# Two graph layers on 128 small graphs: attention weights of the end groups normalised by two engines, one add for two token halves, and new tables for the order of the engines

## The chip, the core and the metric

The kernel runs on one core of a Trainium2 chip. A core has a matrix engine (TensorE, PE in the profile, with its weight loads as PEld), VectorE (DVE), ScalarE (ACT), GpSimd (POOL), and SyncE (SP), whose queue issues the DMAs here. TensorE writes to PSUM[...]. The metric is the device time of one execution in microseconds (us); lower is better.

## The reference, cut to what matters

128 graphs of 128 nodes with 256 features, all fp32, go through two layers. The first has two graph attentions, a layer norm, a feed-forward network and another layer norm; the second has eight-head attention masked by relation, a projection, a layer norm, a feed-forward network and a layer norm.

```python
# layer 0: twice _gat, then layer norm, feed-forward, layer norm
Wh = jnp.matmul(h, W)
e = jax.nn.leaky_relu(Wh @ a1 + swap(Wh @ a2))
att = softmax(where(adj > 0, e, -9e15), axis=1)
h = jnp.matmul(att, Wh)
ff = relu(h @ w_ff1 + b_ff1) @ w_ff2 + b_ff2
# layer 1
attn = softmax(q @ k.T / sqrt(32), axis=-1)
out = sum over r of (attn * (adj == r)) @ v_r
x = _ln(src + out @ Wo + bo)
ff = gelu(x @ W1 + b1) @ W2 + b2
return _ln(x + ff)
```

`adj` holds only 0 and 1. The kernel counts that on the chip and takes a branch for it: two relations instead of four.

## The kernel before, in words

**Tiling.** The 128 graphs make 32 groups of four. In each group one graph's 128 nodes lie on the 128 partitions; `y` is a tile of 128 x 4 x 256. A token of the code below (index `b` or `j`) is one of the four graphs of a group. A group passes five stages: `load` (DMAs of the transposed input `xt` and the mask `at`), `gat` (two graph attentions and a normalisation), `ff0`, `att` (eight heads, two graphs at a time) and `ff1` with the store. Affine parts of the layer norms are applied on GpSimd (L591).

**Feed-forward.** Both products are done as seven block products (the Strassen-Winograd scheme), each part with sums made by VectorE and GpSimd. The first product (L658) runs in two units of four visits each: u0a, u0b, u1a, u0c and so on. A visit ends with an add on VectorE (L665, L674, L675) and a copy on ScalarE (L664, L669, L670) of the same PSUM bank, which a later visit writes again. The second product (L714) adds its results to `y` through `add` (L719) in seven steps; the last is added to both halves of the output columns of tokens 2 and 3. Then `normalised` follows: bn_stats (L577), bn_aggr (L578), an epsilon add (L580), a power on GpSimd (L582), the negative mean (nmr, L583), and four scaled copies on ScalarE (L585).

**Attention weights.** For two graphs at a time the scores (L849) go to PSUM, VectorE takes the row maxima (L853), ScalarE the exponentials with their sums (L862), VectorE the reciprocals (L864), and GpSimd multiplies the 128 x 1024 tile `e` by them (L865). Then `e` is transposed: in the middle groups through VectorE's 32 x 32 transpose (L608) and DRAM, by four stores (L611) and one load (L617) on SyncE's queue; in groups 0 and 31 (`direct`) on TensorE (L602), with copies out of PSUM by ScalarE (L606) and VectorE (L604). The feature tiles `T` are turned in the same two ways. The mask multiply (L884) follows on VectorE, the weighted sums (L913) and the output product (L940) on TensorE.

**Graph attention.** `gat_weighting` needs one column of `wh` as a row on every partition: VectorE transposes it (`zs`, L761), SyncE stores it (`zsd`, L763) and loads it back on all partitions (L766). ScalarE adds the column (L769), VectorE does the leaky step (L776), the mask (L777) and the maximum (L778), ScalarE the exponentials (L781), VectorE the reciprocal (L782), GpSimd the multiply (L783). `cap` (L789) is the compare of the mask.

**What sets the order.** Each stage is a generator that yields between steps. `run` takes the steps of all groups from a heap by their times: a period of 100 per group, a `begin` for each stage, and a list of waits (`steps`). Instructions on TensorE and SyncE keep the order of their steps. Each instruction on VectorE (V), ScalarE (S) and GpSimd (G) has a lag of its own in a table; sorting by step time plus lag gives the order in which its engine gets it, and this order is fixed by dependencies. The numbers are only for sorting: they are not device time. Groups 0 and 31 have tables of their own. A first part, with its own table (`PREFIX`), does the graph attention of groups 0 to 2 and the first feed-forward of group 0, prepares weights, and scans the adjacency (L1113 on ScalarE, L1116 on VectorE); at its end a flag is read and the branch is taken, near 95 us of the profile.

Of the kernel before, what the change touches and what calls it, by code (L numbers as in the profile page):

```python
# [25 lines left out]
G = 4  # L26
# [25 lines left out]
    begin=dict(load=-119.75, gat=-11.95, ff0=94.95, att=174.9, ff1=347.7),  # L52
    steps=dict(
        load=(
            84.25,
        ),
        gat=(
            3.6, 5.8, 1.7, 17.4, 23.25, 4.55, 12.25, 11.5, 16.85,
        ),
        ff0=(  # L60
            1.45, 19.1, 6.85, 4.85, 5.95, 3.1, 5.95, 0.1, 0.3, 0.5, 0.6, 0.4, 0.3, 0.25, 17.5, 0.2,
            0.3,
        ),
        att=(
            2.8, 17.5, 4.45, 19.45, 0.15, 0.55, 0.35, 31.6, 22.6, 0.3, 0.45, 2.45, 5.7, 22.3, 14.15,
# [3 lines left out]
            19.2, 2.9, 3.6, 3.85, 8.5, 0.35, 2.45, 2.05, 0.25, 2.8, 0.15, 1.7, 0.35, 17.9, 4.1, 1.65,  # L69
            37.65, 48, 8, 5.75,  # L70
# [3 lines left out]
        (-2, "ff1"): -2, (-1, "load"): -2, (-1, "ff1"): -5, (3, "load"): 24, (-4, "load"): -10,  # L74
        (4, "load"): -7, (5, "load"): -1, (-5, "load"): -6,
# [3 lines left out]
V 15.2 | S 104.7 95  # L79
S 102.8 104.1  # L80
V 99.9
|
V 102.7 104.7 105.4 117.1 | S 110.4 110.8 110.6 106 112.8 113.3 111.3 112.7 | G 113.4
S 97.7 98.3 99.6 100.4
V 96.7
|
V 84.8 85.6 88.4 99.3 | S 84.3 87.2 88.1 86.4 96.8 90.8 90.2 98.2 | G 102.7
V 91.7 93 92.1 92.3 93.3 95.1 96.7 97.9 98 98.2 98.4 98.6 | S 102.1 99.8 99.4 97 | G 100.7
""",
        "ff0": """  # L90
V 95.8
|
G 92.7 103.2 97.6 110.4
V 107.9 | S 107.3
S 104.3 104.8
V 102.9 | S 103.6 | G 54.9 67.7
V 103.6 104.5
S 98.8 100.9 | G 48.3 50.9
S 103.9 99.6 100.9 105 102.3 98.5
V 101.1 103.3  # L100
S 104.4 106.1 105.3 105.9 106.7 104.2
|
V 101.6 104.3 | G 106.4 100.5
V 105.4 107 | G 110.3
V 105.3 108.1 108.5 | G 104.5
V 96.3 97.5
V 100.9
V 104.4 105.5 100.6 101.4 101.5 106 106.2 107 106.6 107.1 107.3 108.7 | S 111.8 112.5 114.6 110.7 | G 107.2
# [4 lines left out]
V 106.7 105 | S 102.9 114  # L113
V 103.9 106.2 107.4 108.2 110.6 117.5 | S 110.9 112.3 112.9 114.7 113.6 116 115.6 116.9 116.9 121.2 117.3 119.6 120.1 120.9 119.5 120.3 | G 110.5 119.3
V 96.6 103
|
V 110.5 112 | G 55.4 67
V 122.1 129.6
V 105.4 105.6 107.4 107.6 111.5 115.5 | S 104.5 107 108.4 107.3 108.7 108.8 109.6 109 109.9 110.5 114.3 113.2 113.6 110.2 112 113.5 115.4 | G 111.2 116.4
V 97  # L120
V 92.1 95.8
|
V 96.8 98.8 | G 9 14.1
V 106.8 108.6
S 119.4
V 105.5
V 45.9 54.2 50.8 59.3 99.3 99.9 99.7 100 100.5 102.8 | S 103.8 104 105.6 104.7 | G 97.4
""",
        "ff1": """
V 87.7  # L130
|
G 96.4 96.4 111.7 103.9
V 94.9 | S 93.9
S 100.6 92.2
V 92.8 | S 93.3 | G 48.2 62.3
V 96.3 103
S 93.3 93.9 | G 43.6 51.8
S 101.5 102.2 96.5 102.9 90.8 104.9
V 98.6 101.8
S 102.4 102.7 102 102.9 99.4 101.4  # L140
|
V 100 107 | G 92.1 106.8
V 99.7 111.4 | G 101
V 94.7 96 99.5 | G 92.2
V 97.3 100.3
V 101.3
V 65.3 67.6 64.2 64.3 66.8 68.5 70.1 72.5 70.2 72.4 74.1 75.6 | S 77.5 80.2 78.3 76.4 | G 70.5
G 34.5 80.5
G 45.7 46.4
""",  # L150
        "ff0 -1": """
V 100.1 | S 97.2
|
G 71.5 75.6 91.9 103.7
V 109.3 | S 106.9
S 104.2 106.8
V 102.4 | S 101.1 | G 68 76.2
V 105.3 101.8
S 95.4 97.11 | G 59 72.5
S 96.8 99 101.8 104.5 101.3 96  # L160
V 100.8 102.3
S 107.5 110.3 110 110.3 104.5 105.8
|
V 99.5 101.1 | G 102 107.7
V 104.2 109.7 | G 112.9
V 109.6 110.6 113.1 | G 107
V 100.1 101.3
V 101.17
V 103.9 105.7 100.99 102.2 102.1 102.6 105.9 107.2 106.1 106.48 107.8 111 | S 105.12 106.3 106.55 106.8 | G 111
""",  # L170
        "att 0": """
V 119.5 111.85 113.2 113.3 114.4 120.5 116.2 114.8 103.4 109.5 120.6 128.2 107.7 119 112.8 | S 142.2
|
V 105.3 103.7 | S 125.3 129.53
V 105.7 111.1 113 113.3 116.2 119.6 | S 125.46 125.69 125.91 126.9 126.6 126.6 126.82 127.28 127.05 129 127.2 128.2 127.5 128.9 128.64 128.87 | G 109.3 111.2
V 102.2 109.9 | S 110.35 118.1
|
V 103 112.3 | G 66.7 80.2
V 101.7 115
V 102.6 105.9 106.2 107.57 109.2 120.2 | S 98.4 101.2 103 100.3 100.9 102.6 106.3 104.6 111.7 104.4 107 113.3 114 107.7 114.3 115.1 116.9 | G 105.5 121.2  # L180
V 95.8
V 97.05 108.1 | S 102.7 120.3
|
V 104.6 115 | G 12.3 13.3
V 99.4 100
S 112
V 101.3
V 43.7 48 44.1 52.4 95.45 96.2 95.8 97.5 98.61 104.5 | S 105 109.5 109.2 108.7 | G 97
""",
        "att -1": """  # L190
V 101.6 | S 108.7
|
V 106.8 95.7 | S 101.3 101.8
V 103.2 105.6 106 106.5 112 115.8 | S 98.6 102.7 101.6 103.7 104.7 107.8 105.8 110.9 107.4 111 111.5 120 113.1 116.2 112.1 113.7 | G 111 115.6
V 99.3 101.74 | S 102.6 106.2
|
V 108.3 110.8 | G 60.1 61.3
V 99.2 102.1
V 90.2 93.7 96.7 103.7 104.7 107.2 | S 84.3 90.9 95.5 90.7 93.8 102.6 104.2 94.9 98.5 104.3 107.4 97.6 105.2 104.5 110.1 106.8 111.4 | G 90.7 96.2
V 85.8  # L200
V 98 89.3 | S 90.1 93
|
V 95.3 110.7 | G 2 6.7
V 89.8 103.6
S 93.9
V 101.8
V 43.19 53 43.6 45.4 97.3 101.93 101.85 102 102.5 103.1 | S 84.8 87.7 94 104.3 | G 92.5
""",
        "ff1 0": """
V 86.9  # L210
|
G 89.9 91.7 101 107.5
V 94.2 | S 94.56
S 90.9 93.8
V 96 | S 95 | G 48.8 53.4
V 95.6 96.2
S 92.3 92.4 | G 51.8 70.9
S 96 90.2 96.2 99.3 98.6 99.8
V 97 99.3
S 100.6 94.6 96.6 107.6 97.6 102.6  # L220
|
V 97.7 106 | G 103.9 100.1
V 103.5 107.5 | G 104.6
V 94 94.8 98.6 | G 94.1
V 96.2 97.2
V 100.1
V 66.5 68 67.5 70 67.8 71.2 70.8 71.4 71.72 72 73.9 76.4 | S 77.48 75.9 78.2 91.5 | G 70
G 39.2 54.7
G 38.6 59.9
""",  # L230
        "ff1 -1": """
V 83 | S 82.9
|
G 64.85 66.7 68.1 68
V 57.9 | S 65.5
S 62.5 62.1
V 48.2 | S 57.5 | G 40.1 53.8
V 48.8 54
S 68.4 77 | G 44.4 56.4
S 61.7 69 76.2 84.3 53.5 56.1  # L240
V 50.8 53.65
S 82.5 85.1 81.8 86.4 82.1 77.2
|
V 44.6 46.9 | G 61 83.5
V 52.7 53.4 | G 83.6
V 33.7 37.4 40.5 | G 64.3
V 37.4 41.6
V 40.6
V 4.1 9.9 7.3 9.6 10.8 15.3 13.43 15.1 18.9 20.3 20.1 23.4 25.6 28.1 27.3 28.4 32.8 32.9 | S 28.5 26.1 31.7 40.8 | G 33.8 58.3
# [8 lines left out]
            1, 0.05, 6.05, 15.05, 16.05, 3.55, 10.05, 0.05,  # L258
        ),
        (  # L260
            2, 5.55, 4.05, 20.55, 34.5, 0.05, 47, 54.5,
        ),
        (
            31, 0.55, 17, 9.55, 19.5, 3.55, 36, 17.55,
# [4 lines left out]
            69, 10.05, 17.05, 6.05, 10.05, 2.55, 14.05, 1.05, 3.05, 21.55, 12.55, 25.5, 7, 24.55,  # L269
            0.55, 23.05, 4.55, 47.05,  # L270
# [3 lines left out]
        14.5, 97, 35,  # L274
    ),
    scans=(
        34, 39.75, 6.05, 33.25, 5.05, 21.05, 9.55, 19.25, 27.55, 11.55, 13.25, 8.55, 3.55, 1.55,
        4.05, 65.25, 46.05,
# [3 lines left out]
V 2 | S 16.4 3  # L282
S 9.2 4.3
|
V -15.1 -13.2 -1.6 -1.2 -0.7 -0.6 1.2 2.6 | S -4.6 -4.6 -4.6 -3.5 -1.9 -1.5 0 -1.5 | G 3 6.9
S -13.8 -11.9 -11.6 -10.3
|
V -14.6 -13.7 -12.8 -12.7 -12.4 -9.6 -9.7 -8.2 | S -22.4 -18.4 -16.6 -15.6 -13.4 -12.4 -9.4 -9.5 | G -22.2 -20.9
V -6.8 -5.6 -4.9 -3.6 -4 -3.2 -2.6 -1.8 -2.2 -1.8 -1.4 0.8 | S 0.5 0.6 3.2 3.3 | G -4.5
""",  # L290
        (0, 1): """
V 17.1 | S 14.6 16.2
S 11.3 12.6
|
V -7 -3.6 0.1 1.5 4.6 5.5 8 9 | S -9 -8 -7.5 -7 -0.2 -2.2 6.8 5.2 | G 11.3 13.8
S -20.8 -19.7 -20.6 -18.7
|
V -61.8 -60.3 -60 -59.7 -59.1 -58.1 -53.9 -46.9 | S -64.8 -64.3 -64.3 -62.8 -56.9 -55 -56.7 -53.6 | G -48.1 -42.3
V -84.5 -84.3 -83 -82.6 -83 -80.8 -81.2 -79.4 -79.3 -78.9 -75.9 -65.9 | S -66.6 -82.5 -61.4 -79.8 | G -75
""",  # L300
        (0, 2): """
V 15.7 | S 4.4 -1
S 3 6.1
|
V -9.2 -8.5 -7 -8 -6.6 -6.3 -3.8 -2.2 | S -13.6 -12.1 -11.5 -10.3 -7.9 -7 -1.8 -6.3 | G -10.5 -1.1
S -19.8 -19.5 -18.7 -18.3
|
V -52.3 -47.6 -46.8 -47.9 -47.2 -46.9 -44 -40.5 | S -57 -53.7 -53.7 -52.7 -44.2 -43.7 -42.8 -44.8 | G -52.7 -46.2
V -55.8 -53 -52.8 -52 -52.4 -50.2 -51.1 -50.8 -50.7 -49.5 -49.2 -44.6 | S -50.3 -33.2 -37.1 -41.5 | G -56.3
""",  # L310
        (1, 0): """
V -11.8 | S -11.8
|
G -35.3 -34.3 -33.4 -32.6
V -35.2 | S -36.1
S -45.8 -44.8
V -42.6 | S -44.7 | G -56.2 -55.6
V -55.4 -54
S -55 -54.5 | G -69.2 -57.6
S -57.4 -58.1 -56.2 -50.1 -55.1 -57.6  # L320
V -75 -73.7
S -87.6 -85.9 -84.1 -83.2 -85.1 -85.1
|
V -119.7 -116.8 | G -126.8 -118.6
V -136.2 -134.6 | G -132.5
V -135.8 -135.7 -135 | G -134.7
V -155.9 -155.1
V -157.4
V -194.8 -191.1 -196.4 -194.2 -195.5 -191 -190.4 -189.1 -189.5 -189 -180.8 -180.6 | S -192.8 -195.1 -193 -182.4 | G -198.9
""",  # L330
        (2, 0): """
V 11.9 13.1 11 13.3 14.7 19.9 15.7 18.2 18.9 19 24.5 21.7
V -53.6 -43.2 -42 -24.2 -47.9 -40.1 -32.2 -32.5 -40
""",
        (3, 0): """
|
V -34.5
S -44
V -69.8
S -77.1  # L340
V -83.5
S -105.3
V -123.1
S -130.4
V -149.7
S -155.3
V -151.6
# [863 lines left out]
```

## Time and profile before

| | us |
|---|---|
| median of three runs | 2702.02 (2701.94 to 2702.38) |
| the profiled execution | 2707.46 |
| its span, first to last instruction | 2705.6 |
| TensorE busy | 2638.0 |
| VectorE busy | 2090.2 |
| GpSimd busy | 1675.0 |
| ScalarE busy | 1638.7 |
| mean granted clock of TensorE | 0.985 |

The profiled execution lies 5.4 us above the median of the others, so a difference that is worked out from it is taken within it and then set against the median. Of the span, TensorE is without work for 67.6 us. The busy time of TensorE is the union of matmuls that overlap, so a pause of some tenths of a microsecond between two of them does not show in it; the distance from start to start does show it. In the rows of the order of time the columns are the start, the duration, the engine, line, operation and operands, how many are merged, and in brackets the idle time before it with what ended it.

### The profile page before, as it was taken

To read this page: it belongs to the slowest core of one execution; us is meant where nothing else is said; L and a number is where in the kernel's file an instruction comes from. 1 tells how busy PE (TensorE), PEld (TensorE's weight loads), DVE (VectorE), ACT (ScalarE), POOL (GpSimd) and SP (SyncE) were. 2 spreads that over 40 slices of the span, in tenths; PEclk is the share of its full clock that TensorE was granted. 3 is DMA by queue.
4 is the path that set the end of the run, shared out by engine and by line. 5 is a ranking of instruction groups with operands and counts; after the bars stand their busy time and mean duration, and the time that the engine had idled before them with its cause. 6 is when DMAs were issued, how large, how long until landed. Compare 5 with 4: busy or idle time off the path is not lost.

```text
span 2705.6 us, 54054 instructions
## 1 busy us (share of the span) xinstructions
PE 2638.0 (98%) x19686; PEld 2181.8 (81%) x19686; DVE 2090.2 (77%) x3922; ACT 1638.7 (61%) x4957; POOL 1675.0 (62%) x1354
## 2 busy tenths in 40 slices
PE   7789999999999999999999999999999999999997
PEld 5668888888888888888888888888888888888767
DVE  5657887787887788888788888778788778788654
ACT  5346666656666666666666666665666665665543
POOL 2435676667566667666666666666656666766654
PEclk8899999999999999999999999999999999999999
DMA  8125555655655655655655555565554565555310
GB/s 301 33 59 133 114 112 132 139 119 130 128 106 122 149 126 118 131 116 115 140 130 119 133 117 113 133 139 118 131 127 105 125 148 126 115 123 113 77 46 24
DMA packets 1137579, 323.71 MB, mean 120 GB/s; under 512 B 886424, under 2 KB 1106072, under 8 KB 1137176
## 3 DMA queue, kind: packets, MB, share of 16 engines
q1 hardware_dynamic: 1137304, 320.17, 52.2%
q8 instruction: 157, 2.57, 0.4%
q14 instruction: 118, 0.97, 0.1%
HBM read 192.57 MB, written 127.52 MB: 118 GB/s over the span
## 4 chain that ended last, share of the span: by engine, by line
PE 93%; DVE 4%; ACT 2%; issue 1%; POOL 1%; DMA 0%; POOLq 0%; SPq 0%; ACTq 0%; DVEq 0%
PE mm L658 29%; PE mm L714 29%; PE mm L899 8%; PE mm L794 4%; PE av L913 4%; PE mm L833 4%; PE mm L828 4%; PE mm L940 4%; PE mm L849 3%; PE mm L802 2%; PE mm L813 2%; ACT e L862 1%; PE mm L602 1%; PE mm L490 0%; DVE st L577 0%
## 5 line engine op out<-in xcount | busy, mean ns | idle before, releaser
L591 POOL TENSOR_TENSOR y<-y,ln_rows 128x512 f32<-128x512 f32 x508 | 712.2, 1422 | 136.3 <-DVE T L608 118.6
L862 ACT ACTIVATE e<-mm,nm 128x128 f32<-128x128 f32 x1024 | 363.0, 379 | 117.9 <-DVE nm L853 115.1
L582 POOL TENSOR_TENSOR rstd<-rstd,mhalf 128x4 f32<-128x4 f32 x129 | 130.5, 1012 | 387.9 <-DVE rstd L580 377.8
L585 ACT ACTIVATE y<-y,nmr,rstd 128x256 f32<-128x256 f32 x512 | 272.8, 594 | 84.2 <-DVE nmr L583 83.7
L693 POOL TENSOR_TENSOR fT<-fT 128x512 f32<-128x512 f32 x128 | 187.6, 1474 | 170.1 <-DVE sum L691 170.1
L865 POOL TENSOR_TENSOR e<-e,s 128x1024 f32<-128x1024 f32 x128 | 243.0, 1899 | 64.7 <-DVE s L864 54.3
L719 DVE TENSOR_TENSOR y<-y,mm 128x256 f32<-128x256 f32 x512 | 205.5, 402 | 72.8 <-PE mm L714 72.6
L714 PEld LDWEIGHTS mm<-w,fT 128*128 128x128 f32 x2048 | 238.7, 192 | 20.6 <-issue 20.3
L714 PE MATMUL mm<-w,fT 128*128 128x128 f32 x2048 | 247.4, 277 | 0.0
L714 PE MATMUL mm<-wf,fT 128*128 128x128 f32 x2048 | 244.4, 275 | 0.6 <-DVE other L1144 0.6
L714 PEld LDWEIGHTS mm<-wf,fT 128*128 128x128 f32 x2048 | 238.8, 192 | 2.4 <-POOL fT L693 0.8
L899 PE MATMUL mm<-wv,T 128*128 128x512 f32 x512 | 232.3, 597 | 0.0
L862 ACT ACTIVATION_READ_ACCUMULATOR e<-mm,nm 128x1 f32 x1024 | 223.8, 219 | 0.0
L853 DVE TENSOR_REDUCE nm<-mm 128x4 f32<-128x512 f32 x256 | 163.5, 681 | 71.4 <-PE mm L849 71.4
L781 ACT ACTIVATE e<-e,nm 128x128 f32<-128x128 f32 x256 | 103.3, 404 | 169.8 <-DVE nm L778 169.5
L577 DVE BATCH_NORM_STATS2 st<-y 128x6 f32<-128x256 f32 x512 | 201.9, 411 | 3.4
L679 ACT ACTIVATE fT<-fT,col 128x512 f32<-128x512 f32 x256 | 181.4, 725 | 26.7 <-DVE fT L675 26.7
L664 ACT COPY fT<-mm 128x512 f32<-128x512 f32 x128 | 75.8, 592 | 190.8 <-PE mm L658 190.8
L658 PE MATMUL mm<-T,w 128*128 128x256 f32 x768 | 183.6, 382 | 0.3 <-ACT T L606 0.3
L658 PE MATMUL mm<-T,wf 128*128 128x256 f32 x768 | 182.5, 381 | 0.0
L608 DVE STREAM_TRANSPOSE e<-e 128x1024 f32<-128x1024 f32 x120 | 149.1, 1243 | 35.2 <-POOL e L865 34.1
L899 PEld LDWEIGHTS mm<-wv,T 128*128 128x128 f32 x512 | 98.0, 192 | 96.4 <-issue 93.0
(166 smaller groups left out, 6264.5 us busy)
## 6 DMA issues: line engine op xcount, KB each, us to landing
zd<-e SPq DMA_DIRECT2D x480, 128.0 KB, 3.2
eT<-zd SPq DMA_DIRECT2D x120, 512.0 KB, 5.2
zd<-T SPq DMA_DIRECT2D x364, 128.0 KB, 3.3
T<-zd SPq DMA_DIRECT2D x91, 512.0 KB, 4.2
xt<-in_xT_dram SPq DMA_DIRECT2D x32, 512.0 KB, 3.8
y<-in_x_dram SPq DMA_DIRECT2D x32, 512.0 KB, 6.4
out_dram<-y SPq DMA_DIRECT2D x31, 512.0 KB, 5.7
e<-zsd SPq DMA_DIRECT2D x58, 256.0 KB, 4.3
```

Of the source, the lines that this page charges most:

```text
L577: nc.vector.bn_stats(st, y[:, b])
L585: nc.scalar.activation(y[:, b], y[:, b], AF.Identity, bias=nmr[:, b:b + 1], scale=rstd[:, b:b + 1])
L591: engine.tensor_tensor(y[:, b:b + n], y[:, b:b + n], v[:, None, :].to_broadcast([P, n, D]), op)
L658: nc.tensor.matmul(p[:, i], win[k][:, ts(f0 + i, P)], hs[k], start=first and i == 0, stop=True, skip_group_check=True)
L679: nc.scalar.activation(lo[:, i], lo[:, i], func, bias=bin_[:, f0 + i:f0 + i + 1])
L693: nc.gpsimd.tensor_sub(a21, a11, a21)
L714: nc.tensor.matmul(p[:, j], parts[u][k][:, i, ts(j, N)], wout[k][:, 2 * u + i], start=id(bank) not in done, stop=True, skip_group_check=True)
L719: nc.vector.tensor_add(v, v, p)
L853: nc.vector.tensor_reduce(nm.rearrange("p j i -> p (j i)"), p.rearrange("p j i n -> p (j i) n"), AX.X, OP.max, negate=True)
L862: nc.scalar.activation(e[:, k], p[:, j, i], AF.Exp, bias=nms[q][:, j, i:i + 1], accum_out=s[:, k:k + 1])
L865: nc.gpsimd.tensor_mul(e, e, per_row(s, N))
L899: nc.tensor.matmul(p, hT[:, b, f], wv[:, f], start=f == 0, stop=f == DC - 1)
```

## The change

Three edits. First, in `feed_forward` the last product is added to both halves by one instruction over 128 x 512 elements, with the product repeated by a broadcast, instead of two instructions over 128 x 256. Second, in `weights`, in groups 0 and 31 the multiply of the second of the two graphs goes to VectorE; the first one stays on GpSimd, and in all other groups both do. Third, all tables of times and lags have new values. The number of waits and of lag entries changes only where an instruction goes away or moves to another engine.

```diff
         if by < G:
             normalised(y, tag, 0, by)
-        for n in range(2):
-            add(high[:, n], chain)
+        add(high, chain[:, None].to_broadcast([P, 2, 2, D // 2]))
         normalised(y, tag, G - by, by)
...
                 nc.vector.reciprocal(s, s)
-                nc.gpsimd.tensor_mul(e, e, per_row(s, N))
+                if direct and j:
+                    nc.vector.tensor_mul(e, e, per_row(s, N))
+                else:
+                    nc.gpsimd.tensor_mul(e, e, per_row(s, N))
```

The begins and steps of the main part (the k-th number of a list is the wait after the k-th step):

```diff
-    begin=dict(load=-119.75, gat=-11.95, ff0=94.95, att=174.9, ff1=347.7),
+    begin=dict(load=-113.5, gat=-6.2, ff0=100.2, att=180.45, ff1=352.7),
...
-            3.6, 5.8, 1.7, 17.4, 23.25, 4.55, 12.25, 11.5, 16.85,
+            5.85, 3.55, 10.45, 8.15, 23.5, 3.05, 9.25, 15, 17.85,
...
-            1.45, 19.1, 6.85, 4.85, 5.95, 3.1, 5.95, 0.1, 0.3, 0.5, 0.6, 0.4, 0.3, 0.25, 17.5, 0.2,
-            0.3,
+            4.95, 16.85, 6.35, 4.6, 6.2, 3.35, 4.2, 0.6, 0.05, 0.75, 1.85, 0.15, 0.3, 0.15, 17.3,
+            0.2, 0.3,
...
-            19.2, 2.9, 3.6, 3.85, 8.5, 0.35, 2.45, 2.05, 0.25, 2.8, 0.15, 1.7, 0.35, 17.9, 4.1, 1.65,
-            37.65, 48, 8, 5.75,
+            10.2, 7.15, 9.1, 3.85, 8.5, 0.6, 2.2, 2.3, 0.25, 3.05, 0.1, 1.5, 0.05, 17.3, 4.5, 2.15,
+            37.65, 48.75, 4.5, 5.5,
```

In the same way the 16 waits of `att` are changed; their sum goes from 151.75 to 152.2, so its last step, the normalisation, stands at 332.65 instead of 326.65. Within that step the lag of the power on GpSimd goes from 97.4 to 94.4.

Of the lag tables, the lines for the first visits of `ff0` (the third line is the sums on GpSimd, the fourth is u0a with L665 and L664) and the last step of `ff1` (its first numbers are the adds, then bn_stats and bn_aggr in turn):

```diff
-V 95.8
-|
-G 92.7 103.2 97.6 110.4
-V 107.9 | S 107.3
+V 97.3
+|
+G 92.7 101.7 98.1 120.9
+V 107.4 | S 107.3
...
-V 65.3 67.6 64.2 64.3 66.8 68.5 70.1 72.5 70.2 72.4 74.1 75.6 | S 77.5 80.2 78.3 76.4 | G 70.5
+V 67.6 63.7 63.8 65.3 68 70.6 73 71.7 73.4 74.1 74.6 | S 77.5 79.2 77.3 77.4 | G 68
```

Of the first part, the times of group 0's graph attention and of the sixteen scans:

```diff
-            1, 0.05, 6.05, 15.05, 16.05, 3.55, 10.05, 0.05,
+            0, 0.05, 4.55, 18.05, 16.55, 4.55, 8.05, 0.05,
...
-        34, 39.75, 6.05, 33.25, 5.05, 21.05, 9.55, 19.25, 27.55, 11.55, 13.25, 8.55, 3.55, 1.55,
-        4.05, 65.25, 46.05,
+        31.5, 42.25, 1.55, 37.75, 7.55, 19.55, 7.05, 20.75, 20.55, 18.55, 15.25, 3.05, 6.55, 3.05,
+        3.55, 60.75, 49.05,
```

The other lines of the tables, those of groups 0 and 31 and of the first part are changed in the same way, most numbers by some units. The time of the load of group 3 moves from 24 units before its place to 3 after it.

## The prediction

> **What bounds the kernel now.** I read the totals first, then a table by stage, then TensorE's own waits, then the order of time around each wait.
>
> ```profile
> span 2705.6 us, 54054 instructions
> ...
> PE 2638.0 (98%) x19686; PEld 2181.8 (81%) x19686; DVE 2090.2 (77%) x3922; ACT 1638.7 (61%) x4957; POOL 1675.0 (62%) x1354
> ...
> PEclk8899999999999999999999999999999999999999
> ```
>
> TensorE is the bound and its clock is full except at both ends. The table by stage (length, busy us per engine, granted clock, DMA) says where it is not:
>
> ```profile
> 0.00:135.30 135.30, 103.90 (x488) 81.56 (x489) 82.17 (x190) 61.16 (x187) 46.15 (x49) 0.82 0.47 167
> 135.30:340.00 204.70, 193.46 (x1417) 156.88 (x1416) 145.61 (x268) 117.87 (x364) 107.70 (x86) 0.97 0.48 104
> 340.00:2435.00 2095.00, 2094.57 (x15838) 1738.13 (x15837) 1692.70 (x3125) 1322.97 (x4009) 1369.70 (x1097) 1.00 0.57 125
> 2435.00:2600.00 165.00, 159.72 (x1298) 131.25 (x1297) 116.57 (x220) 93.46 (x283) 99.16 (x81) 0.99 0.41 90
> 2600.00:2695.60 95.60, 85.78 (x652) 73.63 (x651) 47.92 (x105) 41.01 (x113) 50.35 (x41) 0.93 0.08 20
> ```
>
> Idle: 31.4 us to 135, 11.2 to 340, 0.4 in 2095 us of the middle, 15.1 from 2435 to 2695.6, then a tail of 10 us. In the middle one group of four tokens takes 80.34 us (the chain repeats so). But "busy" hides short stalls, because matmuls overlap. The order of time shows one in every group (TensorE, then VectorE):
>
> ```profile
> 1007.08 1.89 PE L658 MATMUL mm<-T,wf 128*128 128x256 f32 x8
> 1008.92 2.14 PE L658 MATMUL mm<-t,wf1s 128*128 128x256 f32 x8
> 1010.90 1.46 PE L658 MATMUL mm<-T,wf 128*128 128x256 f32 x6
> ...
> 1008.47 0.68 DVE L583 SCALAR_TENSOR_TENSOR nmr<-mv,rstd 128x4 f32<-128x4 f32 x1 [0.48 <-POOL rstd L582]
> ...
> 1009.23 0.65 DVE L665 TENSOR_TENSOR fT<-fT,mm 128x512 f32<-128x512 f32 x1
> ```
>
> Eight such matmuls need 1.73 us start to start (2485.48 to 2487.20, for example). Here they take 1.84 and 1.98: 0.36 us lost. The second eight write the bank that L665 is still reading until 1009.88.
>
> **How I read the change.** The tables give each instruction a time (step time plus lag); sorted, they are the engines' queues. I sorted both. TensorE's order is the same throughout, but for one swap: the last attention's output product (L940) now follows the "56" products of group 30's second feed-forward. So matmul work is unchanged; only waits can change, by the order on VectorE, ScalarE, GpSimd and SyncE.
>
> **1. The stall of each group.** Before, L665 of the first half unit stood behind two bn_aggr (L578), and nmr (L583) ran beside GpSimd's L638 (1008.41, 0.73 us): 0.68 us, against 0.15 to 0.17 elsewhere (1011.68). After, that L638 sorts to 542.9, behind the feed-forward's rstd power (531.2; before: 525.9 against 527.7), and L665 sorts to 535.75, ahead of the bn_aggr at 536.15 (before: 530.25 behind 529.55 and 529.65). Then nmr ends near 1008.6, and L665 starts when its input is there, near 1008.85 (the ScalarE copy L664 ends 1008.78), and ends 0.65 later at 1009.5, ahead of the 1009.8 at which TensorE wants the bank. The 0.11 us on the copy stays. Of 0.25 I take 0.2 for a slower restart; some 28 groups: **5.6 us**. Ends: 0 (something else arrives at 1009.8) and 28 x 0.36 = 10.1.
>
> **2. Normalisation by two engines.** In groups 0 and 31 the second token's e goes from GpSimd (L865, mean 1899 ns) to VectorE (nearest row L884, 128x1024 from two SBUF operands, 1297 ns): four places.
>
> ```profile
> PE mm L602 <- POOL e L865: 16.0, 4, 7.9
> PE mm L602 <- ACT y L585: 10.6, 3, 3.9
> ...
> PE mm L940 <- ACT oT L917: 4.3, 2, 3.1
> PE mm L658 <- ACT fT L664: 3.7, 1, 3.7
> ```
>
> (TensorE's waits: us, times, longest.) Of the 16.0 us, 11.9 (7.95 at 126.1, 3.98 at 2626.0) is for the first token, which stays on GpSimd. The second token's share is 3.57 at 167.7 and 0.47 at 2628.5; the weight loads show another 0.53 at 128.2 and 0.25 at 2606.
> A rule speaks against counting it all. The row first: L884 took 1.71 us while GpSimd ran L637 and L636, and L638 behind it 1.59 instead of 0.73:
>
> ```profile
> 128.78 0.73 POOL L636 TENSOR_TENSOR t<-T,t 128x256 f32<-128x256 f32 x1
> 128.88 1.71 DVE L884 TENSOR_TENSOR m<-eT,am 128x1024 f32<-128x1024 f32 x1
> 129.58 1.59 POOL L638 TENSOR_TENSOR t<-t,T 128x256 f32<-128x256 f32 x1
> ```
>
> The Trainium skill, "SBUF — State Buffer", section "Who interferes with whom": a VectorE instruction with two SBUF inputs and a GpSimd instruction that reads SBUF exclude each other; the later one waits for the whole of the earlier. Without it the places give 0.5 + 1.05 + 0.25 + 0.5 = 2.3 us. With it: at 126 the next GpSimd work (L635, now behind the first multiply) starts at 126.1, before VectorE's reciprocal ends at 126.15, so the product ends near 128.0 instead of 128.13: 0.1. At 2626 a 1.28 us affine (L591) is next on GpSimd, and one more exponential (0.34) goes ahead of the first token's last: 0. At 2602 VectorE waits for the first multiply until 2604.1: 0.25. At 160 GpSimd is free: before, the reciprocal stood behind a PSUM copy that waits for TensorE (164.9), and the product ended at 167.66; now it follows the L941 add and can end at 166.6: 1.05. I take the rule: **1.4 us**, ends 0 and 2.3. Behind the new multiply stand VectorE's eT copies, which wait for that product anyway.
>
> **3. One add for both halves.** Two L719 adds take 0.75 us (the x2 at 2696.22), one 128x512 add from PSUM 0.68 (L941): 0.07 us, some 60 times beside TensorE's work. In the last group nmr waits for GpSimd's power until 2696.91, so nothing comes of it there; before the branch at 92 it is 0.07 on the path. **0.1 us.** Only one operand is in SBUF.
>
> **4. The order at the ends.** From 0 to 135: a scan (L1113, 1.19 us at 37.2) stood ahead of the fourth row add and all exponentials of group 0's second softmax, for which TensorE waits at 37 to 42; it moves behind them: 1.0. The mask compare and two leaky steps move behind group 0's rstd (49.4; 1 us earlier), for which TensorE waits 2.9 at 52.6: 1.0. A 1.21 us scan (85.96) moves behind an add (87.08) that frees a PSUM bank: 0.6 at 87.6. A weight scaling fills a wait at 105: 0.6. From 135 to 340, SyncE's queue:
>
> ```profile
> 188.55 0.38 SPq L617 DMA_DIRECT2D T<-zd  x1
> 189.04 0.67 SPq L763 DMA_DIRECT2D zsd<-zs  x1
> 192.73 0.34 SPq L766 DMA_DIRECT2D e<-zsd  x1
> ```
>
> The row zs was ready at 181.9, but its transfer stood behind T's load, which waits for T's four stores. Now it goes first (103.2 against 105.15; before 97.45 against 96.4) at about 184.6, and e lands near 192.3 instead of 196.0. ScalarE and VectorE are then busy until 194.4 and 196.6, so VectorE's 1.93 us step at 197.39 (beside a GpSimd multiply) starts ahead of that multiply and takes its 0.6. TensorE's 3.7 us at 203.2 shrinks by 2.2. In the middle the swap is covered: T landed at 1071 is wanted at 1087. From 2435: ScalarE's copy L670 at 2501.96 stood behind a normalisation waiting for nmr and now stands before it: 0.7 of 1.4. At 2563 the transposes and the second add before rstd (2565.41) are reordered; rstd comes at 2564.7, nmr no longer stands behind L941 and a bn_stats, and ScalarE starts at 2566.1 instead of 2568.0: 1.9 of the 3.75 at 2568.65. At 2663 two bn_stats move ahead of the last add: 0.4 of 3.9, the swap of L940 included. Head 5.4, tail 3.0, with parts 2 and 3 together **9.9 us**.
>
> **The sum.** 9.9 at the ends is read with everything else held still; what is gained early is partly lost to the next late input, so I take 0.6 of it, 5.9. With 5.6 in the middle: 11.5 us. Against the profiled execution, 2707.46 (span 2705.6 and 1.9 around it), that is 2696.0. It stands 5.4 above the median of 2702.02; from the median, **2690.5 us**. No wait is removed that lets the 10 us tail after TensorE shrink.
>
> **Rivals.** (A) The middle keeps its stall (another input arrives just as late) and only the ends gain: 2702 - 5.9, cut by a third for order effects, 2698. For it: the 80.34 us repeat unchanged in 26 groups. Against: both causes of the lateness are moved. 14%. (B) Slower: VectorE's q steps and the mask compare L789 now precede zs's transpose and the second unit's sums in every group. If the mask (issued 1059.42) lands after VectorE reaches L789 (near 1065.4, before 1066.95), all behind it wait. VectorE has 2.09 us idle at 1070.5; a lateness beyond that goes on TensorE 28 times. It decides from 0.6 us over (28 x 0.6 = 17 us, which eats 11.5 and 5.4 more): about 2710. Loads of 3.8 us (xt's median) make it unlikely: 6%. (C) Everything fits: 10.1 in the middle, 9.9 at the ends and 2 us of half-clock time: 2680. 13%. (D) The forecast: 67%, own range 2684 to 2696.
>
> **Chances.** 0.2% (5.4 us) is about what a measurement of this kernel can tell from no change. Faster by more: D, C and a few hundredths of A: 0.82; within: most of A, 0.12; slower: B, 0.06. The range takes in D, most of A and the near part of C: 2682 to 2699.
>
> **What would show it.** Right: the pair of eights at L658 starts 1.75 to 1.85 apart, the period falls to about 80.1, nmr there takes 0.15, zsd is issued before T's load, and the waits at 167.7, 203.2 and 2568.6 shrink. Wrong: a period of 80.34 or more, a new wait of TensorE between 340 and 2435, or VectorE's new multiply at 1.9 us or more in all four places.

## The result and the profile after

| kernel | median us (runs) | profiled execution us | its span us |
|---|---|---|---|
| before | 2704.83 (20) | 2707.46 | 2705.6 |
| after | 2697.40 (20) | 2698.19 | 2696.4 |

The ratio of after to before is 0.9975, with a 95% interval of 0.9968 to 0.9982: 6.8 us less (4.9 to 8.7). The forecast was a gain of 11.5 us. The time itself, 2697.4, lies in the range given (2682 to 2699). The three runs of the kernel before that were shown first had a median of 2702.02; the larger sample is 2.8 us higher. The kernel before takes one of two times in most executions (of the 51 runs beside the first timed experiments, 19 take under 2703.6 us, at a mean granted clock of 0.987, and 23 over 2706, at 0.985), and its median lies between the two, so a difference of one or two microseconds can come from how many of each were drawn.

The totals of the changed kernel's page, and then the table by stage (length, busy us per engine, granted clock, DMA share and rate), cut at the same times as before:

```profile
span 2696.4 us, 53995 instructions
...
PE 2631.7 (98%) x19686; PEld 2180.4 (81%) x19686; DVE 2055.0 (76%) x3862; ACT 1631.6 (61%) x4957; POOL 1649.2 (61%) x1350
...
PEclk8899999999999999999999999999999999999999
```

```profile
0.00:135.30 135.30, 104.39 (x502) 82.53 (x503) 83.41 (x191) 62.66 (x191) 44.67 (x48) 0.86 0.47 167
135.30:340.00 204.70, 193.57 (x1420) 155.87 (x1419) 149.41 (x269) 117.69 (x365) 111.48 (x89) 0.98 0.49 106
340.00:2435.00 2095.00, 2094.92 (x15958) 1743.41 (x15956) 1654.69 (x3077) 1318.47 (x4026) 1354.31 (x1099) 1.00 0.57 125
2435.00:2600.00 165.00, 161.04 (x1239) 132.63 (x1238) 115.69 (x217) 94.78 (x285) 94.52 (x77) 0.99 0.40 86
2600.00:2686.00 86.00, 76.83 (x571) 65.20 (x570) 46.23 (x94) 35.77 (x90) 42.26 (x37) 0.92 0.10 25
```

TensorE is still the bound. From 135 to 340 it is idle 11.1 us, as before (11.2). The 2095 us of the middle hold 15958 matmuls in place of 15838; since the cut falls on other places of the program and matmuls differ in length, this is no measure of the gain, which is the period below.

The stall of each group, in the order of time (start, length, engine, line; in brackets the idle time of the engine before and what ended it):

```profile
1001.81 1.89 PE L658 MATMUL mm<-T,wf 128*128 128x256 f32 x8
...
1002.93 0.59 ACT L664 COPY fT<-mm 128x512 f32<-128x512 f32 x1 [3.59 <-PE mm L658]
1003.02 0.16 DVE L583 SCALAR_TENSOR_TENSOR nmr<-mv,rstd 128x4 f32<-128x4 f32 x1 [0.48 <-POOL rstd L582]
...
1003.66 2.02 PE L658 MATMUL mm<-t,wf1s 128*128 128x256 f32 x8
1003.81 0.69 DVE L665 TENSOR_TENSOR fT<-fT,mm 128x512 f32<-128x512 f32 x1 [0.62 <-PE mm L658]
...
1005.52 1.24 PE L658 MATMUL mm<-T,wf 128*128 128x256 f32 x5
```

nmr (L583) takes 0.16 us in place of 0.68, and L665 now waits 0.62 us for TensorE, not for its own engine. Yet the two eights stand 1.85 and 1.86 us apart, not 1.73: 0.25 us is still lost, where 0.36 was, and the period is 80.22 us, 0.12 less than 80.34. TensorE's longest waits in the whole execution (us, times, longest), and SyncE's queue at the next group's row:

```profile
PE mm L602 <- POOL e L867: 10.6, 2, 6.8
PE mm L602 <- ACT y L585: 8.5, 4, 3.2
PE mm L827 <- DMA T<-zd: 5.0, 2, 3.5
...
PE mm L942 <- ACT oT L919: 4.5, 2, 2.8
```

```profile
181.51 0.67 SPq L762 DMA_DIRECT2D zsd<-zs  x1
182.37 0.39 SPq L617 DMA_DIRECT2D T<-zd  x1
183.26 0.34 SPq L765 DMA_DIRECT2D e<-zsd  x1
```

The row's store goes ahead of T's load, as read from the tables. But the third wait is new: attention's q product (L827) of group 1 stands 3.5 us for T, which comes through DRAM (1.5 us in the last group are the other of the two).

### The profile page after: what moved, and what is told of

Read it like the earlier page. It is cut to its first block, busy times and chain, and to the rows that moved or that the text cites. A ratio compares the mean times of both kernels' runs of the same rounds, so it can differ in the third digit from the quotient of the medians.

```text
span 2696.4 us, 53995 instructions
## 1 busy us (share of the span) xinstructions
PE 2631.7 (98%) x19686; PEld 2180.4 (81%) x19686; DVE 2055.0 (76%) x3862; ACT 1631.6 (61%) x4957; POOL 1649.2 (61%) x1350
## 4 chain that ended last, share of the span: by engine, by line
PE 94%; DVE 2%; ACT 1%; DMA 1%; POOL 1%; issue 1%; SPq 0%; POOLq 0%; ACTq 0%; DVEq 0%
PE mm L714 29%; PE mm L658 29%; PE mm L901 8%; PE av L915 4%; PE mm L793 4%; PE mm L827 4%; PE mm L832 4%; PE mm L942 4%; PE mm L848 3%; PE mm L801 2%; PE mm L812 2%; PE mm L602 0%; PE mm L490 0%; ACT e L861 0%; POOL y L591 0%
## 5 line engine op out<-in xcount | busy, mean ns | idle before, releaser
L591 POOL TENSOR_TENSOR y<-y,ln_rows 128x512 f32<-128x512 f32 x508 | 698.5, 1396 | 329.6 <-DVE T L608 314.4
L719 DVE TENSOR_TENSOR y<-y,mm 128x256 f32<-128x256 f32 (+1 forms) x448 | 197.1, 446 | 120.4 <-PE mm L714 118.0
L867 POOL TENSOR_TENSOR e<-e,s 128x1024 f32<-128x1024 f32 x124 | 235.7, 1900 | 51.1 <-DVE s L863 48.4
L861 ACT ACTIVATION_READ_ACCUMULATOR e<-mm,nm 128x1 f32 x1024 | 234.7, 229 | 0.0
L664 ACT COPY fT<-mm 128x512 f32<-128x512 f32 x128 | 75.0, 586 | 229.2 <-PE mm L658 229.1
L693 POOL TENSOR_TENSOR fT<-fT 128x512 f32<-128x512 f32 x128 | 177.1, 1384 | 54.3 <-DVE sum L691 54.3
L674 DVE TENSOR_TENSOR fT<-fT,mm 128x512 f32<-128x512 f32 x128 | 87.5, 684 | 126.8 <-PE mm L658 121.5
L658 PE MATMUL mm<-T,w 128*128 128x256 f32 x768 | 183.8, 383 | 0.0
L658 PE MATMUL mm<-T,wf 128*128 128x256 f32 x768 | 181.4, 379 | 0.0
L691 DVE TENSOR_TENSOR sum<-fT 128x512 f32<-128x512 f32 x128 | 153.2, 1197 | 29.1 <-ACT fT L683 23.3
```

The source lines that it names most:

```text
L591: engine.tensor_tensor(y[:, b:b + n], y[:, b:b + n], v[:, None, :].to_broadcast([P, n, D]), op)
L658: nc.tensor.matmul(p[:, i], win[k][:, ts(f0 + i, P)], hs[k], start=first and i == 0, stop=True, skip_group_check=True)
L693: nc.gpsimd.tensor_sub(a21, a11, a21)
L719: nc.vector.tensor_add(v, v, p)
L861: nc.scalar.activation(e[:, k], p[:, j, i], AF.Exp, bias=nms[q][:, j, i:i + 1], accum_out=s[:, k:k + 1])
L867: nc.gpsimd.tensor_mul(e, e, per_row(s, N))
```

## The experiments

Single profiles differ in the head by several us for the same code. So the table cuts each profiled execution at four fixed points of TensorE's program: *front*, from the first product of group 0's softmax (near 31 us) to the first folding product behind the branch (near 96); *behind*, from there to the seventh step of value products (near 360); *middle*, to the seventh last such step; *tail*, to the end. Each figure is a difference of two starts in the trace. The ratio is to runs of the kernel before timed beside each kernel; their medians lie between 2703.98 and 2706.81 us (the last for "the same, add later" and the last row), so differences of some 0.0005 between rows say little. In the last rows the value products stand elsewhere, so *behind* and *middle* are not set beside the others.

| kernel | ratio, 95% interval | period | front | behind | middle | tail |
|---|---|---|---|---|---|---|
| before | 1 | 80.34 | 65.0 | 264.0 | 2047.9 | 297.0 |
| L638 later | one run | 80.22 | 64.7 | 260.9 | 2045.7 | 298.0 |
| L665 earlier | one run | 80.22 | 63.0 | 261.0 | 2044.7 | 298.8 |
| both moves, one run | one run | 80.22 | 63.4 | 260.6 | 2044.7 | 298.0 |
| both moves, timed | 0.9987, 0.9981 to 0.9994 | 80.22 | 65.6 | 261.3 | 2044.8 | 298.2 |
| edits of code alone | 1.0007, 0.9999 to 1.0015 | 80.45 | 63.2 | 263.7 | 2050.8 | 297.2 |
| the same, add later | 1.0002, 0.9994 to 1.0010 | 80.44 | 65.1 | 260.6 | 2050.1 | 297.8 |
| order alone | 0.9986, 0.9979 to 0.9992 | 80.22 | 64.6 | 261.1 | 2045.8 | 297.2 |
| after | 0.9975, 0.9968 to 0.9982 | 80.22 | 63.8 | 261.9 | 2044.6 | 295.4 |
| after, old front | 0.9971, 0.9960 to 0.9982 | 80.22 | 65.1 | 259.3 | 2045.2 | 294.9 |
| after, T by TensorE | 0.9966, 0.9954 to 0.9978 | 80.22 | 64.3 | 256.1 | 2044.6 | 295.5 |
| after, values between | 0.9943, 0.9928 to 0.9957 | 79.97 | 64.6 | | | 295.0 |
| both of these | 0.9942, 0.9929 to 0.9956 | 79.97 | 64.5 | | | 294.1 |
| values and u0d between | 0.9922, 0.9909 to 0.9936 | 79.79 | 62.3 | | | 296.6 |

**The two moves of the middle, apart and together**, in the kernel before:

```diff
-G 92.7 103.2 97.6 110.4
-V 107.9 | S 107.3
+G 92.7 103.2 97.6 115.4
+V 107.15 | S 107.3
```

The last number of the G line is L638's lag, the first of the V line L665's. L638 alone:

> The kernel before with one edit: in the middle groups the GpSimd subtraction L638 (the last moving sum of the next feed-forward) is put behind the power L582 of the second feed-forward and behind the softmax multiply L783; nothing else moves. If the lateness of L665 comes from nmr (L583) running beside L638: nmr falls from 0.68 us to about 0.16, the two bn_aggr follow it, L665 starts near 0.3 us earlier although it still stands behind both, and the group period falls from 80.34 us nearly as far as in the changed kernel (80.22), with the pair of eights at L658 taking 1.84 and 1.90 us. If the place of L665 behind the two bn_aggr is what counts, the period stays at 80.30 or more. By the prediction as written the period would fall by up to 0.2 (to 80.14).

L665 alone:

> The kernel before with one edit: in the middle groups VectorE's add L665 is moved ahead of the two bn_aggr L578 (it stays behind nmr L583); nothing else moves. If nmr beside GpSimd's L638 sets the lateness, L665 still can't start before nmr ends (1009.15 on the clock of the kernel before, against 1009.23), so the period falls by 0.02 to 0.10 us at most. If the two bn_aggr are the cause, it falls by about 0.12 to 80.22, and by the prediction by up to 0.2.

Both:

> Both moves together in the middle groups (L638 later on GpSimd, L665 earlier on VectorE), nothing else of the change. Theory one: these two moves are all that the middle gained; the period is 80.22 us as in the changed kernel, 0.12 below the kernel before, and the middle is about 3.2 us shorter with the ends untouched (about 2701.5 where the kernel before takes 2704.8). The prediction wanted 80.14 and 5.6 us. Rival: other moves of the new order (the additions L902 behind the next transposition) count too; then the period stays above 80.25. In the pair of eights at L658 I expect 1.84 + 1.87 us rather than twice 1.73, with the part that is left lying on ScalarE's copy L664, which nothing here moves.

The period was 80.22 us in all three (the single times, 2702.0, 2700.5 and 2697.6 us beside 2701.7 for the kernel before, scatter too much to add to that). L665 alone did more than I expected of it; its trace, in order of time:

```profile
1001.78 0.73 POOL L638 TENSOR_TENSOR t<-t,T 128x256 f32<-128x256 f32 x1
1001.84 0.69 DVE L583 SCALAR_TENSOR_TENSOR nmr<-mv,rstd 128x4 f32<-128x4 f32 x1 [0.48 <-POOL rstd L582]
1002.26 2.05 PE L658 MATMUL mm<-t,wf1s 128*128 128x256 f32 x8
1002.45 0.68 DVE L665 TENSOR_TENSOR fT<-fT,mm 128x512 f32<-128x512 f32 x1
1003.05 0.23 DVE L578 BATCH_NORM_AGGREGATE mv<-st 128x2 f32<-128x6 f32 x2
```

nmr still takes 0.69 us beside L638, and L665 starts only when nmr is done; what it no longer waits for is the 0.23 us of L578, and that is enough. Either move brings L665 to the point where it holds TensorE up no more than ScalarE's copy does. Together they give nothing further: the two causes that I named are one gain, and half of the edit would have brought it.

**Both moves, timed**:

> The kernel with the two moves of the middle (L638 later on GpSimd, L665 earlier on VectorE), now timed. Theory one: these moves are worth the period alone, 27 groups x 0.12 us = 3.2 us, ratio to the kernel before 0.9988. Theory two: moving L665 also clears TensorE's wait of up to 3.7 us at L658 near 203 us (it was gone in the one look at this kernel), so that about 6 us go, ratio 0.9978, and nearly the whole effect of the change is this one add; the refitting of the ends would then be worth about 1 us in place of the 5.9 predicted.

Measured 0.9987: 3.5 us (1.6 to 5.1), which is theory one, and half of the whole change. Theory two's 0.9978 lies outside the interval. TensorE's wait near 203 was gone here, but not by these moves: with L665 alone it is gone too, and up to there each engine's order is the same in the kernel before and in the kernels with these moves. The wait hangs on ScalarE's row adds; first before, then with L665 alone:

```profile
196.08 1.28 ACT L769 ACTIVATE e<-e,wh 128x128 f32<-128x128 f32 x4 [1.71 <-DMA e<-zsd]
```

```profile
192.29 1.35 ACT L769 ACTIVATE e<-e,wh 128x128 f32<-128x128 f32 x4
```

They start 1.5 us ahead of the first eight at L658 (197.58) in the one and 5.1 ahead (197.38) in the other. The wait was also gone in the two profiles with the edits of code in the old order, and with the new order it was 0.7 us in one profile and 2.3 in another: it comes and goes between executions.

**The edits of code alone, in the old order**: both edits of the diff, the old tables, with the merged add at the first add's place and the multiply right behind its reciprocal.

> The kernel before, in its old order, with the two edits of code alone: the second token's e multiplied on VectorE in groups 0 and 31 (right behind its reciprocal), and one add of the last product to both halves. By the prediction 1.5 us, of which 0.6 stays: ratio 0.9995 with an interval that holds 1. In the trace: VectorE's multiply takes about 1.25 us near 162 us, where GpSimd is idle; TensorE's wait at 167.7 falls from 3.6 to 2.0 to 2.6 us, and the half-clock stretch behind it shrinks. Rival: the multiplies hold up GpSimd's and VectorE's next work, take 1.8 us or more, and the ratio is 1.000 or above.

The ratio, 1.0007, is the rival's, though its interval holds 1, and not by the rival's mechanism: three of VectorE's multiplies took 1.22 to 1.62 us and the last 1.87, and the tail (297.2) lies among those of the old order (297.0 to 298.8). But the period rose by 0.11 us, 27 times 0.11 = 3 us. In the middle groups the merged add is the only edit that acts. VectorE's order, first before, then with the edits:

```profile
1038.89 0.38 DVE L719 TENSOR_TENSOR y<-y,mm 128x256 f32<-128x256 f32 x1
1039.20 0.18 DVE L864 RECIPROCAL s<-s 128x8 f32<-128x8 f32 x1
1039.30 0.12 DVE L782 RECIPROCAL s<-s 128x4 f32<-128x4 f32 x1
1039.34 0.39 DVE L719 TENSOR_TENSOR y<-y,mm 128x256 f32<-128x256 f32 x1
```

```profile
1035.33 0.65 DVE L719 TENSOR_TENSOR y<-y,mm 128x512 f32<-128x512 f32 x1
1035.91 0.18 DVE L863 RECIPROCAL s<-s 128x8 f32<-128x8 f32 x1
...
1037.69 0.40 DVE L580 TENSOR_SCALAR rstd<-mv 128x4 f32<-128x4 f32 x1
```

The reciprocal stood between the two adds, and GpSimd's multiply waits for it. Behind the merged add it comes 0.3 us later. The power on GpSimd, the normalisation, the transposition to T and GpSimd's work behind that follow 0.2 us late, down to the sum L637, which the second feed-forward's product (L658) needs as weights:

```profile
1044.92 0.73 POOL L637 TENSOR_TENSOR T<-T 128x256 f32<-128x256 f32 x1
1045.71 0.73 PEld L658 LDWEIGHTS mm<-T,w 128*128 128x128 f32 x4 [0.24 <-POOL T L637]
```

The weight load waits for L637 in 23 groups between 500 and 2400 us, and in none in the kernel before; the matmuls there start 0.10 us late. To test the add's place, the one of the first feed-forward was moved behind the reciprocals (that of the second kept its place):

```diff
-V 104.4 100.6 101.4 101.5 106 106.2 107 106.6 107.1 107.3 108.7 | S 111.8 112.5 114.6 110.7 | G 107.2
+V 105.5 100.6 101.4 101.5 106 106.2 107 106.6 107.1 107.3 108.7 | S 111.8 112.5 114.6 110.7 | G 107.2
```

> The kernel before with the two edits of code in its old order, as in the run of the edits alone, but with the merged add of the first feed-forward (middle groups) put where the second of its two adds stood, behind the reciprocals, in place of where the first stood. Theory: the edits alone raised the period from 80.34 to 80.45 us because the merged add, 0.65 us in place of 0.38, stood ahead of the reciprocal for which GpSimd's multiply waits; the multiply, the power behind it, nmr, ScalarE's normalisation, VectorE's transposition and the add L902 then ran 0.2 to 0.3 us late, and TensorE found its bank still in use. Behind the reciprocals the add holds nobody up: the period is 80.34 again and the ratio to the kernel before 0.9990 to 1.0000. Rival: it is the merged add's length itself, wherever it stands, or the other edit: the period stays at 80.45 and the ratio at 1.0007.

The theory of the place falls: the period is 80.44 (the ratio, 1.0002, can't tell). The trace shows the other half:

```profile
1036.39 0.20 DVE L863 RECIPROCAL s<-s 128x8 f32<-128x8 f32 x1
1036.51 0.13 DVE L781 RECIPROCAL s<-s 128x4 f32<-128x4 f32 x1
1036.55 0.66 DVE L719 TENSOR_TENSOR y<-y,mm 128x512 f32<-128x512 f32 x1
...
1038.79 0.17 DVE L580 TENSOR_SCALAR rstd<-mv 128x4 f32<-128x4 f32 x1
```

Now the reciprocal is on time, but VectorE's own chain to rstd (L580) runs late: counted to the first matmul of the row that loses the 0.1 us, L580 starts 6.08 us ahead, and 6.25 in the kernel before; the weight load waits for L637 again, in 23 groups. In the old order the first add ran ahead of the reciprocal; one long add has to stand before it or after it, and either way something is late by 0.2 us. The new order has another place for it: there the period is 80.22 with one add and with two.

**The order alone** (the changed kernel with two adds and both multiplies on GpSimd, the second at about its old place in the queue):

> The changed kernel's order without the two edits of code (both e multiplied on GpSimd in groups 0 and 31, the last product added in two instructions). Theory one: in the changed kernel TensorE then waits 3.5 us for attention's T of group 1, whose transfers hang on the first feed-forward and not on the multiply, so the multiply's gain is covered: the ratio stays within 0.0006 of the full change's 0.9975, the wait for T<-zd shrinks to 2 us or less, and the wait of the transposes L602 for GpSimd's e is 3.5 us or more. Rival: what the multiply gained is kept, and this kernel is 1.5 us or more slower than the full change, ratio 0.9981 or above. In both the period of the middle is 80.22.

0.9986: the rival, and theory one's reason falls with it. TensorE waits 2.4 us for e and then 3.2 for T, where I had expected 2 or less: T hangs on the multiply after all.

```profile
163.41 1.89 POOL L865 TENSOR_TENSOR e<-e,s 128x1024 f32<-128x1024 f32 x1
163.47 1.85 DVE L583 SCALAR_TENSOR_TENSOR nmr<-mv,rstd 128x4 f32<-128x4 f32 x1
167.47 1.25 DVE L608 STREAM_TRANSPOSE T<-y 128x1024 f32<-128x1024 f32 x1 [1.72 <-ACT y L585]
```

Beside GpSimd's multiply nmr takes 1.85 us (0.16 in the changed kernel), and T's transposition follows late. Counted from the start of group 0's transposes of e near 160 (L602), q starts after 16.4 us here, 14.8 in the changed kernel and 15.4 in the kernel before.

The tail is 297.2 without the edits and 295.4 with them. TensorE's waits for the second token's e there are 0.5 and 1.8 us without, 0 and 0.4 with, but the last two can't be set side by side: the first token's transposes ran at another clock (1.27 and 1.97 us for the same eight). From the start of these to the start of the second token's it is 3.09 us without and 2.40 with, so the multiply is worth 0.5 + 0.7 = 1.2 us, where I had forecast 0.25.

**The old front** (the tables ahead of the branch put back):

> The changed kernel, with the order of the part ahead of the branch (groups 0 to 2's graph layers, the first feed-forward, scans and folding) put back to that of the kernel before. Theory one: what is gained ahead of the branch goes through, since everything behind the branch starts from there; by the prediction this part was worth 3.2 us (1.0 + 1.0 + 0.6 + 0.6), so the kernel is about 3 us slower than the full change, ratio to the kernel before 0.9986. Rival: scans and scalings that were moved out of the way of one step stand in the way of the next, and the part is worth 1 us or less: ratio 0.9979 or below.

0.9971, no slower than the change: the rival. Over all profiles here the front takes 63.0 to 65.6 us with its old order and 62.3 to 64.6 with the new, means 64.4 and 64.0. TensorE's waits there say how it evens out: for wh (L757) 3.8 us before and 2.9 after, as forecast; for GpSimd's e (L812) 1.8 before and 2.7 after; for y (L602) 2.9 before and, in two places, 3.1 after.

**T of group 1 by TensorE**: eight transposes and two copies instead of VectorE's transposition and two passes through DRAM.

```diff
-        hT = yield from features(y, direct)
+        hT = yield from features(y, direct or g == 1)
```

Its step moves to just ahead of the third graph layer's products.

> The changed kernel, with attention's T of group 1 turned by TensorE (eight transposes ahead of the third graph layer's first products, two copies) in place of VectorE's transposition and the way through DRAM. Theory one: in the changed kernel TensorE waited 3.5 us for this T and then ran 1.7 us longer at half clock, which gave back what the ends had gained before it; with T there in time, less 1.0 us for the transposes, TensorE is 2.5 to 4 us earlier at the value products near 190 us, and 1.5 to 3.5 us of it reach the end: ratio to the kernel before 0.9962 to 0.9970 (the full change: 0.9975). Rival: the next late input takes it all (the copy L664 at 199 us, which stands behind three exponentials of the next graph layer): TensorE's wait there grows from 2.3 to 5 us or more, and the ratio stays at 0.9975.

0.9966, theory one's range, though the interval also holds the change's own ratio; the trace is clearer. TensorE's waits from 130 to 260 us, with this edit:

```profile
PE mm L962 <- ACT oT L939: 2.8, 1, 2.8
PE mm L622 <- DVE mv L598: 2.2, 1, 2.2
PE mm L678 <- ACT fT L684: 0.6, 1, 0.6
...
```

The wait for T is gone, nothing grew in its place, and *behind* takes 256.1 us, where the other kernels take 259.3 to 264.0. Some of that is luck: in this profile the value products in front of q ran at full clock (3.60 us), in the one with the old front at a lower one (5.29), and q's wait for T was 3.5 us in the changed kernel and 1.8 with the old front.

**The value products between the first two eights.** In the changed kernel:

```diff
-            4.95, 16.85, 6.35, 4.6, 6.2, 3.35, 4.2, 0.6, 0.05, 0.75, 1.85, 0.15, 0.3, 0.15, 17.3,
+            4.95, 16.85, 3.75, 7.2, 6.2, 3.35, 4.2, 0.6, 0.05, 0.75, 1.85, 0.15, 0.3, 0.15, 17.3,
...
-V 107.4 | S 107.3
+V 110 | S 109.9
```

> The changed kernel with one further move: the value products L901 of attention go between the first and the second eight of the first half unit (first visit of each later feed-forward 2.6 earlier on the timetable, its copy L664 and add L665 kept at their own times). Theory: the 0.25 us that each group still loses at L658 is the time from the end of a product over the copy or the add back to TensorE (0.26 + 0.59 + 0.14 us) less the 0.86 us of the one product that lies between; with 3.4 us of products between it is gone, the period is 79.97, and the kernel is 27 x 0.25 = 6.7 us shorter than the changed one, ratio to the kernel before 0.9950. Rival: the bank that the value products now take, two places later in the rotation of seven, is still being read, or the product before waits; then the period is 80.2 or more and nothing is gained.

As expected: 79.97, and 0.9943. The lines (one lower than in the changed kernel):

```profile
995.48 1.89 PE L657 MATMUL mm<-T,wf 128*128 128x256 f32 x8
996.60 0.59 ACT L663 COPY fT<-mm 128x512 f32<-128x512 f32 x1
997.21 3.60 PE L900 MATMUL mm<-wv,T 128*128 128x512 f32 x8
...
1000.64 1.89 PE L657 MATMUL mm<-t,wf1s 128*128 128x256 f32 x8
1002.37 2.75 PE L657 MATMUL mm<-T,wf 128*128 128x256 f32 x12
```

The second eight takes 1.73 us to the next start. So the 0.25 us that the change left was never VectorE's order. With T by TensorE on top:

> The kernel with the value products between the two eights (0.9943 before) and in addition T of group 1 turned by TensorE as in the run above. There TensorE still waits 1.9 us for T. Theory one: 1 to 2.5 us more go, ratio 0.9934 to 0.9940, the lowest of all kernels here. Rival: the wait moves to the next input and nothing more goes, ratio 0.9943 within its interval. The period of the middle is 79.97 either way.

0.9942: the rival; no more can be seen, so what T by TensorE is worth stays open. Last, without T by TensorE, the values between and the last product of the first half unit (u0d) between the last two visits of the second (order 0, 0, 1, 0, 1, 1, 0, 1 in the middle groups' first feed-forward, its line of lags with it):

> The kernel with the value products between the first two eights (0.9943, period 79.97) and in addition, in the middle groups' first feed-forward, the last product of the first half unit put between the last two visits of the second, so that both places where a bank is read back within 0.86 us are cleared. Theory: the second 0.25 us goes like the first, period 79.72, 27 x 0.25 = 6.7 us less, ratio 0.9918. Rival: the first products of the second layer (L714) need the activations of the product that now comes later; they wait, and the period stays at 79.97 or rises.

The period fell to 79.79, 0.18 of the 0.25 us expected, and the ratio is 0.9922 (2685.5 us): the fastest kernel of the study, from five runs.

## Why the prediction was right in kind and wrong in size

By the table the change gained 3.3 us in the middle (2047.9 to 2044.6), about 2.7 in the tail (mean 298.0 in the five profiles with the old order and none of the edits, 295.3 in the three with the new order, the edits and the same value steps) and about 1 in the head, the rest of 6.8. The single profiles scatter too much in the head to say more. The forecast had 5.6 for the middle, and after the factor 0.6 about 4.0 for the head and 2.0 for the tail. So of the 4.7 us that it was too high, 2.3 are part 1's and 3 the head's, and the tail gave back 0.7.

- **What bounds it, and that only waits change**: right.
- **Part 1, 0.2 us a group, 5.6 in all**: the mechanism was right (nmr 0.16 us, L665 at its input), the term was mis-sized: 0.12 a group. The sum gave 0.11 of the loss to the copy L664 and 0.25 to L665. The starts of the single matmuls in the kernel before say otherwise: 0.12 + 0.08 at the copy, 0.07 + 0.10 at L665; in both places the lateness of the bank is followed by a second loss, in front of the next matmul. After the change the copy's 0.20 is untouched and 0.06 is left at L665. The copy can't be in time: the product ends at 1002.67 (1001.81 + 0.86), the copy starts 0.26 later and ends at 1003.52, and TensorE, due at 1003.54, starts at 1003.66. Rival A's worry, another input just as late, was true of more than half of the stall.
- **Part 2, 1.4 us by the rule**: the four multiplies took 1.61, 1.21, 1.22 and 2.21 us. The last shows the exclusion:

```profile
2617.56 1.27 POOL L591 TENSOR_TENSOR y<-y,ln_rows 128x512 f32<-128x512 f32 x1
...
2617.69 2.21 DVE L865 TENSOR_TENSOR e<-e,s 128x1024 f32<-128x1024 f32 x1
```

 VectorE's multiply, issued 0.13 us into GpSimd's affine, takes 1.0 us longer than near 162, where GpSimd is idle. The rule held, and so did the 0 at this place against the old order. What failed is the rest: of the 1.05 at 160 about 0.6 is left when q starts (14.8 us for 15.4), since q waits for T, and at 2600 to 2623 the multiply is worth 1.2 us in the new order, not 0.25.
- **Part 3, one add, 0.1 us**: mis-read. The saving on VectorE was there (0.65 us for 0.77), but in the old order it cost 3 us over the middle, since it is one block where two fitted around a reciprocal. The new order hides that.
- **Part 4, head 5.4**: the step that failed. Of the 3.2 us up to 135, the front came to about 0.4, because the wait for GpSimd's e grew as that for wh shrank, and that for y, from which I had taken 1.0, stayed. Of the 2.2 us at 203, SyncE's order was read rightly, but the wait fell only from 3.7 to 2.3. I had VectorE's step start ahead of GpSimd's multiply and take 0.6 us; in the changed kernel it starts 0.5 us after the multiply (193.04) and takes 1.93:

```profile
193.56 1.93 DVE L775 SCALAR_TENSOR_TENSOR e<-e 128x512 f32<-128x512 f32 x1 [0.66 <-ACT e L768]
```

 And of the five profiles whose order up to there is that of the kernel before, the wait is missing in three, so less than 3.7 us stood in the median. What was gained at 160 to 167 ran into the new wait of q for T (3.5 us), and the stretch of lower clock only moved: the value products took 5.72 us before and 3.60 after, q 3.60 and 5.37. From the transposes of e near 160 to group 1's scores TensorE takes 22.4 us before, 23.5 after and 21.8 with the old front. I had written that a gain made early is partly lost to the next late input, and kept 0.6 of all; of the head's 6.6 us (with its shares of parts 2 and 3) about 1 came, as what the middle and the tail leave of the 6.8.
- **Part 4, tail 3.0**: right in sum, as far as single profiles tell. The waits for y fell from 7.7 to 5.4 us in two places and the 1.4 at L658 went; a wait of 1.5 for T came.
- **Rivals**: none came as written. The time, 2697.4, is near A's 2698, but by another way: A leaves the middle its stall. B's VectorE queue did not slip in the new order; C was out of reach with the order of products that the change keeps.

Whether each single move in the front gains or loses was not tried; nor was any kernel run with a part of the tail's tables.

## What to carry to other kernels

Before counting a stall to the engine that seems late, take the time from the end of the product over its reader and back to TensorE and set it against the work between: if the work is shorter, no order of the reader's engine helps, but another product in between does. A saved instruction is judged by what stood between the two that it replaces. A gain ahead of a chain through DRAM counts only up to that chain's own arrival, and a wait that hangs on a transfer should be seen in more than one execution before it is put in a sum. Two kernels are compared from start to start of the same instructions, not wait by wait, since a lower clock ahead of a wait shortens it.

## What the runs showed of the hardware

A wait of the same length is followed by a lower clock in one execution and not in another. TensorE's rows with the old front, then with T by TensorE; the transposes have waited 2.23 us in both:

```profile
165.44 1.12 PE L602 MATMUL mm<-ident,e 128*128 128x128 f32 x8 [2.23 <-DVE mv L578]
166.35 5.29 PE L901 MATMUL mm<-wv,T 128*128 128x512 f32 x8
```

```profile
163.87 1.06 PE L622 MATMUL mm<-ident,e 128*128 128x128 f32 x8 [2.23 <-DVE mv L598]
164.77 3.60 PE L921 MATMUL mm<-wv,T 128*128 128x512 f32 x8
```

The same eight products take 5.29 and 3.60 us, at a mean granted clock of 0.67 and 1.00; in the first, the first five start 0.84 to 0.86 us apart, the others 0.43. The Trainium skill, "TensorE: Matmul & The Clock Gate", section "Part 1: The HAM clock gate (the "warmup" mystery)", has the clock judged over a window that runs freely, so that the outcome depends on where in it the work falls; that fits. The section gives an idle stretch of about 3.4 us as what brings the lower clock; here it followed a wait of 2.23 us. The changed kernel's 20 runs spread from 2693.4 to 2703.3 us with a mean granted clock of 0.989 to 0.985: by an estimate from these two, 0.004 of 2700 is 10.8 us, as large as the spread. A change worth 7 us can be seen in medians of many runs, and not in the head of one profile.
